# Storing the softmax statistics of a cross-attention kernel by quarters of the queries

## The chip, the cores and the metric

The kernel runs on one core of a Trainium2 chip. The metric is the device time of one execution in microseconds, as a median over runs. Its five engines are named as in the profile: PE (TensorE matmuls; PEld is its weight loading), DVE (VectorE), ACT (ScalarE), POOL (GpSimd) and SP (SyncE, which here only issues DMAs).

## What is computed

Two decoder layers on `x` of shape (2, 512, 1024), with a context of shape (2, 1024, 1024), all in float32. The first layer adds a quantized matrix product of the normalized `x` with the context, and a linear layer with routed LoRA. The second adds a cross-attention with 32 query heads over 8 key/value heads of width 128, and a linear layer with a top-1 LoRA. The change lies in the cross-attention of the second layer:

```python
q = (query @ wq).reshape(bs, sq, N_Q_HEADS, D_K).transpose((0, 2, 1, 3))
...
raw = jnp.einsum('bhqd,bhkd->bhqk', q, k) / scale
masked = raw + mask[:bs, None, curr_seq_pos:curr_seq_pos + sq, :sk]
attn = jax.nn.softmax(masked, axis=-1)
out = jnp.einsum('bhqk,bhkd->bhqd', attn, v)
out = out.transpose((0, 2, 1, 3)).reshape(bs, sq, N_Q_HEADS * D_V)
return out @ wo
```

With 2 batches and 32 heads there are 64 heads to work through. One has 512 queries and 1024 keys.

## The kernel before

Scores are kept transposed: keys lie on the 128 partitions, queries along the free dimension. A head's scores are eight blocks of 128 keys by 512 queries, in two SBUF tiles `e[0]` and `e[1]` of [128, 4, 512] (blocks, queries). The softmax statistics of a query, its maximum and its sum of exponentials, therefore need a reduction over blocks and then over partitions.

`Head.scores` (L763 to L784) does the products with PE and adds the mask on DVE, out of a two-bank PSUM tile `wide` into `e` (L782). `Head.tree` (L786 to L797) takes the maximum over the eight blocks with four DVE instructions: L790 of two halves of `e[0]` into a tile `m` of [128, 2, 512], L792 and L794 of `m` with the halves of `e[1]`, and L796, which folds `m` to its first [128, 512]. `over_partitions` (L727) finishes the reduction: it turns the 512 columns onto partitions by four PE transposes (L732; the data are PE's weights, the identity is what streams), and one DVE reduction (L734) gives [128, 4] numbers. `to_row` writes these to DRAM so that one transfer can bring them back as a row for all partitions (`from_row`, L747). To have that write in order, query 4p + t has to be at partition p, column t; so `over_partitions` views its input as "p (q t) -> p t q", and transpose number t takes every fourth query. The 128 weight columns of a transpose lie four floats, 16 bytes, apart.

`Head.exponential` (L812) subtracts the maximum on DVE (L814, out of PSUM, where ACT has put it at L810), takes the exponential on ACT (L817), and sums on POOL: for the first half of the keys L820 (`e[0]`'s two halves into a tile `d` of [128, 2, 512]), for the second L823 and L824 (`d` with each half of `e[1]`) and L825, which folds `d` to [128, 512]. `turn_sum` then runs `over_partitions` and a reciprocal (L805); POOL multiplies the result into the head's output at L842 (`normalize`). `Head.attend` (L827) is the product with the values (L831).

The order of all engines in this stage is the order of the program; no scheduler moves anything there. `attention` (L856) is a pipeline over heads with three phases per iteration n. In the first, head n + 2 has its scores made. In the second, PE runs three or four steps of the output projection of the group of four heads that is finished (L355, whose results DVE adds with L322 and L328 and POOL adds with L310), and DVE runs the tree of head n + 2 between those additions. In the third, PE runs in this order: the transposes for head n's sum, half of head n's product with the values, the transposes for head n + 2's maximum, and the other half; DVE, ACT and POOL work through the exponentials of head n + 1. Where a group of four heads is finished, POOL also makes the operands of its projection (`left_sums`, L242, lines L245 to L253). PE waits in its queue wherever a wait comes up, with everything behind it.

The queues: SP issues the loads of q, keys, values, masks and weights, ACT issues the two transfers of `row` (L741, L747).

Of the kernel before, what the change touches and what calls it, by code (L numbers as in the profile page):

```python
# [15 lines left out]
ALU = mybir.AluOpType  # L16
AX = mybir.AxisListType

P = 128
B, S, D = 2, 512, 1024  # L20
# [11 lines left out]
NT = S // P  # L32
# [7 lines left out]
def decoder_kernel(  # L40
# [25 lines left out]
    nc = tc.nc  # L66
# [8 lines left out]
    def new(shape, tag, bufs, dtype=F32):  # L75
        n_tiles[0] += 1
        return sb.tile(list(shape), dtype, tag=tag, name=f"{tag}_{n_tiles[0]}", bufs=bufs)
# [4 lines left out]
    def u4(shape, dtype=F32):  # L82
        return new(shape, "u4", 17, dtype)
# [4 lines left out]
    def small(shape):  # L88
        return new(shape, "small", 16)

    def ps_wide():
        n_tiles[0] += 1
        return ps.tile([P, D], F32, tag="wide", name=f"wide_{n_tiles[0]}", bufs=2)
# [23 lines left out]
    for name, ap in qparams.items():  # L117
        t = const.tile([P, 1], F32, name=f"qp_{name}")
        nc.gpsimd.dma_start(t, ap.partition_broadcast(P))
        qp[name] = t  # L120
    for side in ("x1", "x2"):
        t = const.tile([P, 1], F32, name=f"qp_inv_{side}")
# [603 lines left out]

    def over_partitions(src, op, negate=False):  # L727

        src = src.rearrange("p (q t) -> p t q", t=NT)
        tr = ps_wide()[:, 0:HALF].rearrange("p (t q) -> p t q", t=NT)  # L730
        for t in range(NT):
            nc.tensor.transpose(tr[:, t, :], src[:, t, :], ident)  # L732
        r = small([P, NT])
        nc.vector.tensor_reduce(r, tr, AX.X, op, negate=negate)  # L734
        return r

    def to_row(col):

        n_tiles[0] += 1
        row = dr.tile([S], F32, tag="row", name=f"row_{n_tiles[0]}", bufs=8)  # L740
        nc.scalar.dma_start(row.rearrange("(p t) -> p t", t=NT), col)  # L741
        return row
# [9 lines left out]
    class Head:  # L752
# [32 lines left out]

        def tree(self):  # L786

            e = self.e
            m = self.m = u4([P, 2, S])
            nc.vector.tensor_tensor(m, e[0][:, 0:2, :], e[0][:, 2:4, :], ALU.max)  # L790
            yield
            nc.vector.tensor_tensor(m, m, e[1][:, 0:2, :], ALU.max)  # L792
            yield
            nc.vector.tensor_tensor(m, m, e[1][:, 2:4, :], ALU.max)  # L794
            yield
            nc.vector.tensor_tensor(m[:, 0, :], m[:, 0, :], m[:, 1, :], ALU.max)  # L796
            yield  # L797

        def turn_maximum(self):
            self.nmx = over_partitions(self.m[:, 0, :], ALU.max, True)  # L800
            self.nmx = to_row(self.nmx)

        def turn_sum(self):
            den = over_partitions(self.d[:, 0, :], ALU.add)
            nc.vector.reciprocal(den, den)  # L805
            self.den = to_row(den)

# [4 lines left out]
        def exponential(self, j):  # L812
            e = self.e[j]
            nc.vector.tensor_tensor(  # L814
                e, e, self.nmf.unsqueeze(1).to_broadcast([P, 4, S]), ALU.add
            )
            nc.scalar.activation(e, e, AF.Exp)  # L817
            if j == 0:
                d = self.d = u4([P, 2, S])
                nc.gpsimd.tensor_tensor(d, e[:, 0:2, :], e[:, 2:4, :], ALU.add)  # L820
            else:
                d = self.d
                nc.gpsimd.tensor_tensor(d, d, e[:, 0:2, :], ALU.add)  # L823
                nc.gpsimd.tensor_tensor(d, d, e[:, 2:4, :], ALU.add)  # L824
                nc.gpsimd.tensor_tensor(d[:, 0, :], d[:, 0, :], d[:, 1, :], ALU.add)  # L825

        def attend(self, j):  # L827
            if j == 0:
# [27 lines left out]
    def attention(extra):  # L856
# [28 lines left out]
        for n in range(-2, total + GRP + 1):  # L885
# [30 lines left out]
            for _ in range(3 + k % 2 if n > GRP else 0):  # L916
                next(stretches, None)
                next(tree, None)
# [3 lines left out]
            for _ in range(extra.pop(n, 0)):  # L922
                for _ in range(2):
                    next(tree, None)
                next(extra["products"])
# [469 lines left out]
```

## Time and profile before

| | |
|---|---|
| median of 3 runs | 2449.82 us (2448.38 to 2452.53) |
| profiled execution, its own time | 2450.07 us |
| its span, first to last instruction | 2448.3 us |
| granted TensorE clock | 0.999 |
| PE busy | 2412.5 us (99%) |
| DVE busy | 1841.1 us (75%) |
| POOL busy | 1031.3 us (42%) |
| ACT busy | 530.8 us (22%) |
| L732, the transposes in `over_partitions` | 512, from 948.5 to 2302.7 us |
| L790, first instruction of the tree | 64, median 1.888 us |
| L820, L823, L824, sums of exponentials | 64 each, mean 2.367, 2.354, 2.356 us |

Busy shares are means over the whole span. Here they mix a first part of some 930 us, in which POOL has little to do, with the attention stage, from about 930 to 2310 us, in which POOL is busy 59 us of 83. A PE matmul's recorded duration contains a latency that overlaps with the next matmul, so PE's pace is read from the distance of two starts, or from the chain of waits, and not from the mean duration.

### The profile page before, as it was taken

Reading aid. Unit: us, or ns where it says so; the run is one execution under the profiler, and the core shown is the slowest. Engines: PE = TensorE matmul, PEld = TensorE weight load, DVE = VectorE, ACT = ScalarE, POOL = GpSimd, SP = SyncE. Lnnn points to the kernel's source line nnn. Section 1 sums busy time; section 2 is a strip of 40 time slices with the busy share of each in tenths; the row PEclk is TensorE's granted clock in tenths of the full one; section 3 lists DMA queues with packets and bytes.
Section 4 is the critical chain, followed back from the end, with each engine's and each line's share of the span. In section 5 each row is a group of like instructions: output and inputs, shape, how many; then the busy total and the mean of one; then the engine's idle time right before and its main releaser. Section 6 shows DMA issues by size and latency. Waiting matters only on the chain.

```text
span 2448.3 us, 19583 instructions
## 1 busy us (share of the span) xinstructions
PE 2412.5 (99%) x6792; PEld 1195.8 (49%) x6800; DVE 1841.1 (75%) x1994; ACT 530.8 (22%) x623; POOL 1031.3 (42%) x550
## 2 busy tenths in 40 slices
PE   8999999999999999999999999999999999999999
PEld 3477458654444443444444444444444444444444
DVE  4949774345876556898888888888898998888653
ACT  1210221011222222322222222222222222222210
POOL 0000010210000001677676767667776767677621
PEclk9999999999999999999999999999999999999999
DMA  5537133013796221244323323442433343233501
GB/s 182 181 105 273 69 134 108 26 60 116 274 330 216 78 91 56 77 156 111 81 83 107 114 65 90 142 145 79 125 116 79 94 125 112 66 90 108 172 9 60
DMA packets 149010, 288.01 MB, mean 118 GB/s; under 512 B 29424, under 2 KB 47360, under 8 KB 146608
## 3 DMA queue, kind: packets, MB, share of 16 engines
q1 hardware_dynamic: 108080, 244.35, 29.9%
q10 hardware_dynamic: 40400, 41.70, 6.9%
q8 instruction: 54, 0.88, 0.2%
q0 software_dynamic: 432, 0.71, 0.1%
q14 instruction: 44, 0.36, 0.1%
HBM read 223.54 MB, written 63.18 MB: 117 GB/s over the span
## 4 chain that ended last, share of the span: by engine, by line
PE 60%; DVE 6%; POOL 2%; issue 1%; DMA 1%; ACT 1%; ACTq 0%; SPq 0%; DVEq 0%; POOLq 0%
PE b L355 26%; PE wide L768 16%; PE b L831 15%; PE wide L732 2%; DVE u L814 2%; DMA u<-in_wo_dram 1%; DVE u L782 1%; POOL u L823 0%; POOL u L824 0%; DVE small L734 0%; DVE u L792 0%; DVE u L794 0%; ACT u L817 0%; POOL u L825 0%; DVE u L328 0%
## 5 line engine op out<-in xcount | busy, mean ns | idle before, releaser
L355 PE MATMUL b<-u,u 128*128 128x512 f32 (+1 forms) x3616 | 1394.2, 542 | 21.3 <-DMA u<-in_ctxT_in_dram 7.6
L355 PEld LDWEIGHTS b<-u,u 128*128 128x128 f32 x3616 | 684.6, 191 | 695.9 <-issue 612.8
L768 PE MATMUL wide<-u,u 128*128 128x512 f32 x1024 | 454.8, 595 | 7.3 <-DVE u L782 6.4
L831 PE MATMUL b<-u,u 128*128 128x512 f32 x1024 | 460.3, 592 | 0.0
L782 DVE TENSOR_TENSOR u<-wide,u 128x1024 f32<-128x1024 f32 x256 | 312.8, 1224 | 130.3 <-PE wide L768 129.9
L817 ACT ACTIVATE u<-u 128x2048 f32<-128x2048 f32 x128 | 244.7, 1912 | 655.8 <-DVE u L814 593.9
L768 PEld LDWEIGHTS wide<-u,u 128*128 128x128 f32 x1024 | 193.4, 190 | 257.3 <-issue 177.9
L814 DVE TENSOR_TENSOR u<-u,b 128x2048 f32<-128x2048 f32 x128 | 290.2, 2268 | 0.0
L820 POOL TENSOR_TENSOR u<-u 128x1024 f32<-128x1024 f32 x64 | 151.5, 2367 | 317.5 <-ACT u L817 310.1
L831 PEld LDWEIGHTS b<-u,u 128*128 128x128 f32 x1024 | 186.2, 192 | 184.6 <-issue 184.6
L310 POOL TENSOR_TENSOR u<-u,u 128x512 f32<-128x512 f32 x120 | 188.5, 1597 | 175.4 <-DVE u L322 153.2
L328 DVE TENSOR_TENSOR u<-u,b 128x512 f32<-128x512 f32 x200 | 135.8, 680 | 126.0 <-PE b L355 125.9
L222 POOL TENSOR_TENSOR u<-u,sin_t 128x512 f32<-128x512 f32 x8 | 11.6, 1456 | 402.7 <-ACT u L217 402.7
L823 POOL TENSOR_TENSOR u<-u,u 128x1024 f32<-128x1024 f32 x64 | 150.7, 2354 | 36.4 <-ACT u L817 36.0
L824 POOL TENSOR_TENSOR u<-u,u 128x1024 f32<-128x1024 f32 x64 | 150.8, 2356 | 5.0
L842 POOL TENSOR_TENSOR u<-u,u 128x512 f32<-128x512 f32 x64 | 119.9, 1873 | 10.0 <-DMA u<-row 10.0
L216 ACT ACTIVATE u<-u 64x512 f32<-64x512 f32 x72 | 45.2, 628 | 356.3 <-DVE u L293 177.6
L790 DVE TENSOR_TENSOR u<-u 128x1024 f32<-128x1024 f32 x64 | 115.8, 1810 | 0.0
L732 PEld LDWEIGHTS wide<-ident,u 128*128 128x128 f32 x512 | 79.6, 203 | 63.9 <-issue 55.0
L612 POOL TENSOR_TENSOR u<-u,u 128x1024 f32<-128x1024 f32 x8 | 20.2, 2529 | 214.9 <-DVE u L168 111.6
L792 DVE TENSOR_TENSOR u<-u,u 128x1024 f32<-128x1024 f32 x64 | 105.4, 1646 | 0.2
L825 POOL TENSOR_TENSOR u<-u 128x512 f32<-128x512 f32 x64 | 101.0, 1578 | 5.0
(135 smaller groups left out, 1614.3 us busy)
## 6 DMA issues: line engine op xcount, KB each, us to landing
u<-row ACTq DMA_DIRECT2D x128, 256.0 KB, 3.7
u<-wo SPq DMA_DIRECT2D x64, 512.0 KB, 4.0
u<-in_wo_dram SPq DMA_DIRECT2D x48, 512.0 KB, 4.5
u<-in_wq_dram SPq DMA_DIRECT2D x32, 512.0 KB, 4.2
q<-u SPq DMA_DIRECT2D x64, 256.0 KB, 2.4
u<-in_wo_dram SPq DMA_DIRECT2D x16, 1024.0 KB, 8.2
wo<-u SPq DMA_DIRECT2D x32, 512.0 KB, 4.2
u<-q SPq DMA_DIRECT2D x64, 256.0 KB, 4.2
```

What stands on the lines that cost most here:

```text
L310: nc.gpsimd.tensor_tensor(c, c, what, ALU.add)
L328: nc.vector.tensor_tensor(c, c, acc, ALU.add)
L355: nc.tensor.matmul(acc, lhsT, rhs, start=start and k == 0, stop=k == len(pairs) - 1, skip_group_check=True,)
L732: nc.tensor.transpose(tr[:, t, :], src[:, t, :], ident)
L768: nc.tensor.matmul(sc[:, ts(n, HALF)], self.kT[:, ts(2 * j + n, P)], self.qT, start=True, stop=True,)
L782: nc.vector.tensor_tensor(self.e[j // 2][:, js, :], sc.rearrange("p (k q) -> p k q", k=2), mask[j], ALU.add)
L814: nc.vector.tensor_tensor(e, e, self.nmf.unsqueeze(1).to_broadcast([P, 4, S]), ALU.add)
L817: nc.scalar.activation(e, e, AF.Exp)
L820: nc.gpsimd.tensor_tensor(d, e[:, 0:2, :], e[:, 2:4, :], ALU.add)
L823: nc.gpsimd.tensor_tensor(d, d, e[:, 0:2, :], ALU.add)
L824: nc.gpsimd.tensor_tensor(d, d, e[:, 2:4, :], ALU.add)
L831: nc.tensor.matmul(self.acc, self.v[:, k, :], self.e[j][:, k % 4, :], start=(k == 0), stop=(k == NKT - 1),)
```

## The change

`m` and `d`, the tiles that hold the tree's results and the sums, get the shape [128, 2, 4, 128]: the queries stand in them by quarters, t outermost. A new helper `by_quarter` views `e` in that order, "p k (q t) -> p k t q", and the instructions that read `e` (in the tree the first three, in the sums the first three) now read it with a step of four floats, and write or update `m` and `d` with neighbouring columns. L796 and L825 work on `m` and `d` alone, without gaps. `over_partitions` drops its view and takes `src[:, t, :]` as it stands, so that the 128 weight columns of each transpose are neighbours. The tiles have the same bytes as before, and no instruction is added, dropped or moved.

```diff
     def over_partitions(src, op, negate=False):
-        src = src.rearrange("p (q t) -> p t q", t=NT)
         tr = ps_wide()[:, 0:HALF].rearrange("p (t q) -> p t q", t=NT)
         for t in range(NT):
             nc.tensor.transpose(tr[:, t, :], src[:, t, :], ident)
...
+    def by_quarter(src):
+        return src.rearrange("p k (q t) -> p k t q", t=NT)
...
         def tree(self):
-            e = self.e
-            m = self.m = u4([P, 2, S])
-            nc.vector.tensor_tensor(m, e[0][:, 0:2, :], e[0][:, 2:4, :], ALU.max)
+            e = [by_quarter(half) for half in self.e]
+            m = self.m = u4([P, 2, NT, P])
+            nc.vector.tensor_tensor(m, e[0][:, 0:2], e[0][:, 2:4], ALU.max)
             yield
-            nc.vector.tensor_tensor(m, m, e[1][:, 0:2, :], ALU.max)
+            nc.vector.tensor_tensor(m, m, e[1][:, 0:2], ALU.max)
             yield
-            nc.vector.tensor_tensor(m, m, e[1][:, 2:4, :], ALU.max)
+            nc.vector.tensor_tensor(m, m, e[1][:, 2:4], ALU.max)
             yield
-            nc.vector.tensor_tensor(m[:, 0, :], m[:, 0, :], m[:, 1, :], ALU.max)
+            nc.vector.tensor_tensor(m[:, 0], m[:, 0], m[:, 1], ALU.max)
             yield
...
             nc.scalar.activation(e, e, AF.Exp)
+            e = by_quarter(e)
             if j == 0:
-                d = self.d = u4([P, 2, S])
-                nc.gpsimd.tensor_tensor(d, e[:, 0:2, :], e[:, 2:4, :], ALU.add)
+                d = self.d = u4([P, 2, NT, P])
+                nc.gpsimd.tensor_tensor(d, e[:, 0:2], e[:, 2:4], ALU.add)
             else:
                 d = self.d
-                nc.gpsimd.tensor_tensor(d, d, e[:, 0:2, :], ALU.add)
-                nc.gpsimd.tensor_tensor(d, d, e[:, 2:4, :], ALU.add)
-                nc.gpsimd.tensor_tensor(d[:, 0, :], d[:, 0, :], d[:, 1, :], ALU.add)
+                nc.gpsimd.tensor_tensor(d, d, e[:, 0:2], ALU.add)
+                nc.gpsimd.tensor_tensor(d, d, e[:, 2:4], ALU.add)
+                nc.gpsimd.tensor_tensor(d[:, 0], d[:, 0], d[:, 1], ALU.add)
```

More of the change, by code (lines that the diff above doesn't have):

```diff
@@ L786, in tree @@
         def tree(self):
-            e = self.e
-            m = self.m = u4([P, 2, S])
-            nc.vector.tensor_tensor(m, e[0][:, 0:2, :], e[0][:, 2:4, :], ALU.max)
+            e = [by_quarter(half) for half in self.e]
+            m = self.m = u4([P, 2, NT, P])
+            nc.vector.tensor_tensor(m, e[0][:, 0:2], e[0][:, 2:4], ALU.max)
             yield
-            nc.vector.tensor_tensor(m, m, e[1][:, 0:2, :], ALU.max)
+            nc.vector.tensor_tensor(m, m, e[1][:, 0:2], ALU.max)
             yield
-            nc.vector.tensor_tensor(m, m, e[1][:, 2:4, :], ALU.max)
+            nc.vector.tensor_tensor(m, m, e[1][:, 2:4], ALU.max)
             yield
-            nc.vector.tensor_tensor(m[:, 0, :], m[:, 0, :], m[:, 1, :], ALU.max)
+            nc.vector.tensor_tensor(m[:, 0], m[:, 0], m[:, 1], ALU.max)
             yield
         def turn_maximum(self):
-            self.nmx = over_partitions(self.m[:, 0, :], ALU.max, True)
+            self.nmx = over_partitions(self.m[:, 0], ALU.max, True)
             self.nmx = to_row(self.nmx)
         def turn_sum(self):
-            den = over_partitions(self.d[:, 0, :], ALU.add)
+            den = over_partitions(self.d[:, 0], ALU.add)
             nc.vector.reciprocal(den, den)
```

## The prediction

> **What bounds the kernel now.** I read the page first: engine shares, then the chain of work that ended last.
>
> ```profile
> PE 2412.5 (99%) x6792; PEld 1195.8 (49%) x6800; DVE 1841.1 (75%) x1994; ACT 530.8 (22%) x623; POOL 1031.3 (42%) x550
> PE b L355 26%; PE wide L768 16%; PE b L831 15%; PE wide L732 2%; DVE u L814 2%; DMA u<-in_wo_dram 1%; DVE u L782 1%; POOL u L823 0%; POOL u L824 0%; DVE small L734 0%; DVE u L792 0%; DVE u L794 0%; ACT u L817 0%; POOL u L825 0%; DVE u L328
> ```
>
> PE is the bound; the transposes (L732) are 2% of the chain, and DVE and POOL lines of the softmax appear in it here and there, so they are near it. Next, the chain in order of time, for one head in the middle of attention (start, length, what):
>
> ```profile
> 1503.84 0.47 PE wide L732 x4
> 1504.31 3.44 PE b L831 x8
> 1507.75 0.47 PE wide L732 x4
> 1508.22 3.44 PE b L831 x8
> 1511.65 6.87 PE wide L768 x16
> 1518.52 6.87 PE b L355 x16
> ```
>
> No gap: PE goes from one matmul to the next, and a head lasts 21.54 us (19.83 where the projection has three steps). Whatever PE saves is saved, and whatever makes PE wait is lost in full. So I looked next at how late the two transposes' inputs are. On DVE the tree, then in PE's timeline the transposes of the maximum that wait for it:
>
> ```profile
> 1520.88 1.34 DVE L790 TENSOR_TENSOR u<-u 128x1024 f32<-128x1024 f32 x1
> 1522.74 1.69 DVE L792 TENSOR_TENSOR u<-u,u 128x1024 f32<-128x1024 f32 x1
> 1524.95 1.70 DVE L794 TENSOR_TENSOR u<-u,u 128x1024 f32<-128x1024 f32 x1
> 1527.17 1.16 DVE L796 TENSOR_TENSOR u<-u 128x512 f32<-128x512 f32 x1
> 1529.13 0.63 PE L732 MATMUL wide<-ident,u 128*128 128x128 f32 x4
> ```
>
> The tree ends at 1528.33, 0.80 us before PE takes it. In four heads in a row the same distance is 0.28, 0.47, 0.80 and 0.87 us; the shortest anywhere in the stage is about 0.15, which is the handover itself. That leaves 0.13, 0.32, 0.65 and 0.72 us to spare: DVE has almost none. POOL, before the transposes of the sum at 1503.68:
>
> ```profile
> 1488.58 3.74 POOL L310 TENSOR_TENSOR u<-u,u 128x512 f32<-128x512 f32 x3
> 1492.50 2.37 POOL L820 TENSOR_TENSOR u<-u 128x1024 f32<-128x1024 f32 x1 [0.17 <-ACT u L817]
> 1495.35 2.36 POOL L823 TENSOR_TENSOR u<-u,u 128x1024 f32<-128x1024 f32 x1 [0.48 <-ACT u L817]
> 1497.78 2.35 POOL L824 TENSOR_TENSOR u<-u,u 128x1024 f32<-128x1024 f32 x1
> 1500.21 2.13 POOL L825 TENSOR_TENSOR u<-u 128x512 f32<-128x512 f32 x1
> 1503.68 0.63 PE L732 MATMUL wide<-ident,u 128*128 128x128 f32 x4
> ```
>
> The sum is ready at 1502.34, 1.34 us early, 1.28 beyond a handover of 0.06. The next three heads have 4.09, 2.72 and 4.78. In this head POOL was without work for only 0.17 us before L820: from the previous head's L842 on it had made the projection's operands and three additions.
>
> **What the change takes from PE.** The loads of transposes with neighbouring columns can be seen in the same trace, at L204 (nanoseconds: least, median, most):
>
> ```profile
> L732 PEld LDWEIGHTS wide<-ident,u x512: 195/207/223, 948.5 to 2302.7; 128*128 128x128 f32 x171
> L204 PEld LDWEIGHTS wide<-ident,u x192: 139/141/143, 361.3 to 2382.7; 128*128 128x128 f32 x192
> 361.56 1.04 PE L204 MATMUL wide<-ident,u 128*128 128x128 f32 x8
> 362.43 7.07 PE L355 MATMUL b<-u,u 128*128 128x256 f32 x32
> ```
>
> A load shrinks by 66 ns, which over 512 would be 34 us, but loads overlap matmuls. What counts is pace: L204's eight start 0.87 us before the next matmul, 0.109 each; L732's four take 0.47 on the chain, 0.1175 each. Four save 0.47 - 4 x 0.109 = 0.035 us. There are 128 groups of four: 4.5 us, 0.18% of the span. I bound it at 0 and at 5.5 (a group at 0.427, the pace of 128 columns at a fourth of L831's 0.429 per matmul). Everything else is the price.
>
> **What it puts on DVE.** L790, L792 and L794 read `e` in steps of 16 bytes; L790 does so with both operands. The trace has no such DVE read. Below nothing is excluded: the elements are as many. The nearest row is PE's own: a load of 128 columns 16 bytes apart every 0.1175 us is 0.92 ns per column, while DVE needs 1.02 ns per element (L790's least 1.215 us for 1024, L796's least 0.691 for 512). By that row a stepped read keeps up and the tree costs nothing more. Against it stands the Trainium skill, "SBUF — State Buffer", section "Door 1: The DMA port swizzle": SBUF works in 16-byte lines, and each access that goes to a new line pays a penalty[...]. It gives no price; a doubled stream would be 1.05 us on each of three instructions, X = 3.1 us. PE would then wait X less the spare: 4 x 3.1 - 1.8 = 10.6 us in four heads, 169 us in 64. By the row 0, by the rule up to 169. I take the row, as it is this chip reading with this very step, and keep the other end for the range. The gain is eaten already at X = 0.36 us: (0.36 - 0.13) + (0.36 - 0.32) = 0.27 per four heads, which is what PE saves there (8 x 0.035).
>
> **What it puts on POOL.** L820, L823 and L824 read `e` in the same steps. Again no row shows it; below nothing is excluded in the same way. PE's row would let it pass: POOL takes 2.12 ns per element ((2.355 - 1.271 us) / 512), more than twice 0.92. The rule: the Trainium skill, "GPSIMD Engine Reference", section "7. Performance pitfalls for Q7 kernels": an SBUF read that steps by more than 8 bytes takes about 2.9 cycles per element in place of 1.9. Here I take the rule, since it was measured on this engine and PE's load tells of PE's port alone. One cycle at the page's 1.2 GHz is 0.83 ns: an estimate of 0.85 us for each of the three instructions, Y = 2.55 us per head. Ends: 0, and 7.1 (all three twice as long).
>
> Where this ends, by the four heads: POOL works through the fourth head's sums, then L842, the operands and three additions, and L820 of the next head follows with 0.17 us of slack. So that head gets the delay twice: 2 x 2.55 - 0.17 - 1.28 = 3.65 us of waiting PE. The other three have 4.03, 2.66 and 4.72 to spare and cover 2.55.
>
> There is a second path. DVE and POOL hold each other up when both read two operands from SBUF:
>
> ```profile
> L790 DVE TENSOR_TENSOR u<-u x64: 1215/1888/3348, 939.9 to 2256.3; 128x1024 f32<-128x1024 f32 x64
> ```
>
> The most, 3.35, is the least plus 2.13: it stood behind a POOL instruction. A later L824 now reaches into the tree. In the head shown L790 (1520.88) would wait for L824 to end at 1519.77 + 2.55 = 1522.3 and end near 1523.4 instead of 1522.22: 1.2 late, less 0.65 to spare, 0.5. The next head's L824 ends at 1540.99 + 2.55 = 1543.5, so L790 ends at 1544.6 instead of 1543.41: 1.2 less 0.72, again 0.5. In the fourth L824 ends at 1563.3, where L790 already waited to. Together 1.0. L328, L796 and the subtractions (L814) queue behind the tree on DVE, and ACT's exponentials behind L814, so a late tree delays the next sums too; that is the same wait once more and I don't add it.
>
> Sum: 3.65 + 1.0 = 4.65 us per four heads, times 15 (the first group has no operands to make) = 70; less 4.5: 65 us. Against the profiled execution's 2450.07 (span 2448.3 and 1.8 around it; 0.25 above the median) that is 2515 us.
>
> **No cost.** L796 and L825 stay contiguous and as long. SP's and ACT's transfers are the same: `row` gets the same bytes in the same order. All engines' instructions keep number and place, so no queue is passed and no buffer lives longer, except by the delays above.
>
> **The rivals.** *Nobody pays.* Stepped reads run at full pace on DVE and POOL. Then only the 4.5 us remain: 2445.5. For it: PE's 0.92 ns per column. Against: POOL's page. Chance 0.25. *DVE pays* (alone, or with POOL). 3.1 us more in the tree gives 169 - 4.5: 2615 us; it decides from X = 0.36 on, and in that case POOL's delay lies mostly beside it, since the wait for the sum gives the tree time. With half the price, X = 1.55, (1.42 + 1.23 + 0.90 + 0.83) x 16 = 70. For it: the line rule, and a tree with 0.13 us to spare. Against: PE's row. Chance 0.33. *The change doesn't do what it says*: columns become neighbours but the transposes keep their pace; L204 speaks against it, and it would only take the 4.5 us away.
>
> **How the numbers follow.** POOL alone pays: 0.42, 2515 us, with 2465 to 2600 for Y from 1.5 to 4.7. A measurement of this kernel tells about 0.2%, 5 us, from no change. Nobody pays: its 4.5 lie just within that; I give 0.09 to faster, 0.14 to same and 0.02 to slower. Of POOL's case 0.02 is same (a price under Y = 0.9 stays below PE's gain), 0.40 slower; DVE's 0.33 is slower. Together 0.09, 0.16 and 0.75. The range from 2444 to 2640 takes in the case of no price and DVE's doubled reads; outside lie about 0.04 below and 0.12 above (both engines paying double, each standing behind the other).
>
> **What would show it.** Right: L732's loads at 0.14 us and four transposes at 0.435 on the chain; L820 to L824 at 3.2 us or more; PE waiting for POOL's L825 ahead of the sum's transposes, in every fourth head first, up to 3.6 us; the tree's least times still 1.215. Wrong: L790's least well above 1.3 us (DVE pays, and PE waits for L796 in every head), or L820 still at 2.37 (then only PE's gain is left). It would be wrong in size if both engines are slow and stand behind each other more than I counted.

## The result and the profile after

The changed kernel takes 2707.7 us (median; 2706.2 to 2713.6) against 2449.1 us: a ratio of 1.105, 95% interval 1.104 to 1.107, 258 us slower. The prediction was slower at 2515 us, with a range up to 2640; the time lies outside it. In the changed kernel's lines the transposes are L731, the tree L793, L795, L797 and L799, the sums L824, L827, L828 and L829, POOL's multiplication L846, the product with the values L835, and DVE's subtraction and ACT's exponential L817 and L820.

The page of the changed kernel, span, busy times and the chain that ended last:

```profile
span 2706.9 us, 19591 instructions
PE 2474.1 (91%) x6800; PEld 1202.9 (44%) x6800; DVE 2102.6 (78%) x1994; ACT 530.2 (20%) x623; POOL 1397.2 (52%) x550
PE 31%; POOL 21%; DVE 15%; issue 4%; ACT 2%; DMA 1%; POOLq 0%; ACTq 0%; SPq 0%; DVEq 0%
```

And the chain's shares before:

```profile
PE 60%; DVE 6%; POOL 2%; issue 1%; DMA 1%; ACT 1%; ACTq 0%; SPq 0%; DVEq 0%; POOLq 0%
```

The span grew by 258.6 us. PE is busy 61.6 us longer and idle 197.0 us longer. PE was 60% of the chain before; now POOL and DVE together hold more of it than PE does. The single instructions, from the views of their lines (nanoseconds: least, median, most):

```profile
L731 PEld LDWEIGHTS wide<-ident,u x512: 137/141/231, 946.7 to 2561.3; 128*128 128x128 f32 x171
L793 DVE TENSOR_TENSOR u<-u x64: 1990/3028/4732, 938.2 to 2509.0; 128x1024 f32<-128x1024 f32 x64
L795 DVE TENSOR_TENSOR u<-u,u x64: 2002/2524/4541, 940.2 to 2511.9; 128x1024 f32<-128x1024 f32 x64
L797 DVE TENSOR_TENSOR u<-u,u x64: 2020/2486/2983, 942.3 to 2516.1; 128x1024 f32<-128x1024 f32 x64
L824 POOL TENSOR_TENSOR u<-u x64: 4051/4169/4255, 971.0 to 2547.9; 128x1024 f32<-128x1024 f32 x64
L827 POOL TENSOR_TENSOR u<-u,u x64: 2857/2878/2933, 975.2 to 2552.0; 128x1024 f32<-128x1024 f32 x64
```

The loads shrank as expected, to L204's 141 ns. All three tree instructions need 2.0 us at least where 1.215 did before, whether one operand is stepped or both. POOL needs 1.80 us more where both are (2.367 before) and 0.52 more where one is (2.354). Two rows of the page show what else grew, POOL instructions that the change doesn't touch (busy, mean ns, then idle before):

```profile
L846 POOL TENSOR_TENSOR u<-u,u 128x512 f32<-128x512 f32 x64 | 187.7, 2934 | 11.2 <-DMA u<-row 11.2
L829 POOL TENSOR_TENSOR u<-u 128x512 f32<-128x512 f32 x64 | 160.8, 2513 | 5.0
```

Before, these were 1.873 us (L842) and 1.578 us (L825). They stand behind DVE's longer reads, as the run with the tree alone will show. And PE's transposes, with its idle time ahead of them and who ended it, after and before:

```profile
L731 PE MATMUL wide<-ident,u 128*128 128x128 f32 x512 | 88.2, 299 | 176.4 <-POOL u L829 128.5 <-DVE u L799 44.4 <-DVE u L206 2.0
L732 PE MATMUL wide<-ident,u 128*128 128x128 f32 x512 | 81.8, 282 | 2.7 <-POOL u L825 1.6 <-DVE u L796 0.9
```

The chain in order of time, through one head and into the next (start, length, what):

```profile
1659.86 2.40 DVE u L797
...
1663.71 2.27 DVE u L817
...
1666.00 1.92 ACT u L820
...
1667.99 4.20 POOL u L824
...
1678.17 2.93 POOL u L829
...
1694.99 4.17 POOL u L824
...
1706.81 2.90 POOL u L829
...
1709.75 1.12 PE wide L731 x4
1710.87 5.13 PE b L835 x8
1716.00 0.44 PE wide L731 x4
1716.43 3.44 PE b L835 x8
```

It runs from the tree through the exponential into POOL, through two heads' sums there, and only then to PE. The last four lines show the gain, four transposes in 0.44 us in place of 0.47, and something new: after its wait PE takes 1.12 and 5.13 us for what otherwise takes 0.44 and 3.44. The stretches around that wait have the reason (the columns are busy times, then the granted clock):

```profile
core 0: us, PE busy (x) PEld busy (x) DVE busy (x) ACT busy (x) POOL busy (x), PEclk, DMA share, GB/s
1704.00:1709.70 5.70, 0.00 (x0) 0.00 (x0) 5.70 (x5) 0.00 (x0) 5.62 (x3) 0.79 0.04 14
1709.70:1713.20 3.50, 3.45 (x7) 1.92 (x8) 3.46 (x3) 0.00 (x0) 2.98 (x1) 0.50 0.00 0
1713.20:1716.00 2.80, 2.80 (x8) 1.26 (x7) 2.77 (x4) 0.00 (x0) 0.00 (x0) 0.83 0.03 1
1716.00:1720.00 4.00, 4.00 (x13) 1.99 (x12) 3.11 (x3) 2.52 (x2) 1.76 (x1) 1.00 0.59 123
```

PE's clock falls to half in the wait and stays there for some microseconds of work. That is where most of the 61.6 us of longer busy time are: the products with the values, which follow these waits, alone are busy 44.8 us longer (after, then before):

```profile
L835 PE MATMUL b<-u,u 128*128 128x512 f32 x1024 | 505.1, 640 | 0.0
L831 PE MATMUL b<-u,u 128*128 128x512 f32 x1024 | 460.3, 592 | 0.0
```

### The profile page after: what moved, and what is told of

It is laid out like the page before. It is cut to its first block, busy times and chain, and to the rows that moved or that the text cites. A ratio compares the mean times of both kernels' runs of the same rounds, so it can differ in the third digit from the quotient of the medians.

```text
span 2706.9 us, 19591 instructions
## 1 busy us (share of the span) xinstructions
PE 2474.1 (91%) x6800; PEld 1202.9 (44%) x6800; DVE 2102.6 (78%) x1994; ACT 530.2 (20%) x623; POOL 1397.2 (52%) x550
## 4 chain that ended last, share of the span: by engine, by line
PE 31%; POOL 21%; DVE 15%; issue 4%; ACT 2%; DMA 1%; POOLq 0%; ACTq 0%; SPq 0%; DVEq 0%
PE b L355 14%; PE wide L771 7%; PE b L835 7%; POOL u L824 5%; POOL u L828 4%; POOL u L827 4%; DVE u L795 3%; DVE u L797 3%; POOL u L829 3%; DVE u L817 2%; POOL u L310 2%; ACT u L820 1%; DVE u L328 1%; POOL u L846 1%; PE wide L731 1%
## 5 line engine op out<-in xcount | busy, mean ns | idle before, releaser
L355 PEld LDWEIGHTS b<-u,u 128*128 128x128 f32 x3616 | 683.1, 191 | 719.1 <-issue 605.1
L835 PE MATMUL b<-u,u 128*128 128x512 f32 x1024 | 505.1, 640 | 0.0
L820 ACT ACTIVATE u<-u 128x2048 f32<-128x2048 f32 x128 | 244.6, 1911 | 902.7 <-DVE u L817 865.5
L824 POOL TENSOR_TENSOR u<-u 128x1024 f32<-128x1024 f32 x64 | 266.8, 4169 | 253.5 <-ACT u L820 253.5
L835 PEld LDWEIGHTS b<-u,u 128*128 128x128 f32 x1024 | 203.0, 209 | 213.0 <-issue 213.0
L817 DVE TENSOR_TENSOR u<-u,b 128x2048 f32<-128x2048 f32 x128 | 290.1, 2268 | 0.0
L310 POOL TENSOR_TENSOR u<-u,u 128x512 f32<-128x512 f32 x120 | 200.2, 1694 | 174.0 <-DVE u L322 152.9
L731 PE MATMUL wide<-ident,u 128*128 128x128 f32 x512 | 88.2, 299 | 176.4 <-POOL u L829 128.5
L328 DVE TENSOR_TENSOR u<-u,b 128x512 f32<-128x512 f32 x200 | 136.1, 681 | 125.4 <-PE b L355 120.1
L828 POOL TENSOR_TENSOR u<-u,u 128x1024 f32<-128x1024 f32 x64 | 225.9, 3530 | 5.0
L793 DVE TENSOR_TENSOR u<-u 128x1024 f32<-128x1024 f32 x64 | 199.6, 3119 | 0.0
L795 DVE TENSOR_TENSOR u<-u,u 128x1024 f32<-128x1024 f32 x64 | 195.8, 3059 | 0.2
L846 POOL TENSOR_TENSOR u<-u,u 128x512 f32<-128x512 f32 x64 | 187.7, 2934 | 11.2 <-DMA u<-row 11.2
L827 POOL TENSOR_TENSOR u<-u,u 128x1024 f32<-128x1024 f32 x64 | 184.3, 2879 | 5.3 <-ACT u L820 0.4
L731 PEld LDWEIGHTS wide<-ident,u 128*128 128x128 f32 x512 | 63.4, 151 | 261.2 <-POOL u L829 155.8
L829 POOL TENSOR_TENSOR u<-u 128x512 f32<-128x512 f32 x64 | 160.8, 2513 | 5.0
L797 DVE TENSOR_TENSOR u<-u,u 128x1024 f32<-128x1024 f32 x64 | 158.8, 2481 | 0.1
```

Source lines behind the costliest of these rows:

```text
L310: nc.gpsimd.tensor_tensor(c, c, what, ALU.add)
L355: nc.tensor.matmul(acc, lhsT, rhs, start=start and k == 0, stop=k == len(pairs) - 1, skip_group_check=True,)
L795: nc.vector.tensor_tensor(m, m, e[1][:, 0:2], ALU.max)
L817: nc.vector.tensor_tensor(e, e, self.nmf.unsqueeze(1).to_broadcast([P, 4, S]), ALU.add)
L824: nc.gpsimd.tensor_tensor(d, e[:, 0:2], e[:, 2:4], ALU.add)
L827: nc.gpsimd.tensor_tensor(d, d, e[:, 0:2], ALU.add)
```

## The experiments

The theory after the result: DVE and POOL both pay for reads in steps of 16 bytes, the two prices add, and PE's half clock adds to them. The rival: POOL alone pays, as predicted, and DVE's longer times are waiting behind POOL.

**The tree alone.** Only DVE reads by quarters.

```diff
-            e = by_quarter(e)
...
-                d = self.d = u4([P, 2, NT, P])
+                d = self.d = u4([P, 2, S])
...
-            den = over_partitions(self.d[:, 0], ALU.add)
+            den = over_partitions(self.d[:, 0, :], ALU.add, turned=False)   # views it "p (q t) -> p t q"
```

> Only the tree's three instructions on DVE read by quarters; the sums on POOL and their transposes are as before. Theory (DVE and POOL both pay for reads in steps of 16 bytes, 0.79 us more for each DVE instruction of 1024 elements): the tree takes 2.4 us more, of which about 0.45 was to spare, so PE waits near 1.9 us per head, about 120 us in 64 heads, and POOL's instructions that stand behind a DVE read get longer: 2550 to 2600 us. Rival 'POOL alone' (DVE's longer times in the changed kernel are only waiting behind POOL): DVE's least times stay 1.215 us and the time is 2447 to 2455 us.

Measured: 2577.0 us, ratio 1.052 (1.050 to 1.053), 127 us more. The tree's first instruction, and POOL's multiplication (L842 before, least 1.258, median 2.248 us):

```profile
L795 DVE TENSOR_TENSOR u<-u x64: 1996/2541/4079, 940.1 to 2381.4; 128x1024 f32<-128x1024 f32 x64
L847 POOL TENSOR_TENSOR u<-u,u x64: 1267/3072/3131, 1008.1 to 2440.0; 128x512 f32<-128x512 f32 x64
```

DVE needs 2.0 us with POOL reading as before: the price is DVE's own, 0.78 us per instruction, and the rival falls. By the prediction's own account, X = 2.37 (0.775 + 0.784 + 0.81) less the spare, 4 x 2.37 - 1.82 = 7.66 us per four heads, gives 123 us in 64, or 121 after PE's gain of 2.2 in its 64 shorter groups. The total fits better than its parts: in the trace PE waits 80.6 us for the tree itself,

```profile
PE wide L733 <- DVE u L801: 80.6, 55, 4.2
```

(us in all, times, longest), and 13.1 us more for DVE's additions (L328), which stand in DVE's queue among the tree's instructions. POOL's multiplication is 1.8 us over its least where it stands behind a DVE read; before it was 1.0. With its own instructions unchanged, POOL is busy 1177.1 us here for 1031.3.

**The sums alone.** Only POOL reads by quarters.

```diff
-            e = [by_quarter(half) for half in self.e]
-            m = self.m = u4([P, 2, NT, P])
+            e = self.e
+            m = self.m = u4([P, 2, S])
...
-            self.nmx = over_partitions(self.m[:, 0], ALU.max, True)
+            self.nmx = over_partitions(self.m[:, 0, :], ALU.max, True, turned=False)
```

> Only the sums on POOL read by quarters; the tree and the maximum's transposes are as before. Theory: POOL takes 1.80 + 0.52 + 0.53 = 2.85 us more per head; by the prediction's own account 2 x 2.85 - 1.45 = 4.25 us of waiting in every fourth head and about 1.2 through the tree, 15 groups, 80 us, and some more if PE's clock falls after the waits: 2525 to 2560 us. Rival 'POOL alone': nearly all of the 258 us is here, 2690 us or more. If the two effects only lay beside each other, this would be near the changed kernel less a few us.

Measured: 2573.3 us, ratio 1.050 (1.049 to 1.052), 123 us more. So each price is there alone, and they add to 127 + 123 = 250 of 258; the rival, which has nearly all of it here, falls again. PE's wait in every fourth head, in its timeline:

```profile
1461.71 1.12 PE L733 MATMUL wide<-ident,u 128*128 128x128 f32 x4 [4.13 <-POOL u L831]
1462.62 4.61 PE L837 MATMUL b<-u,u 128*128 128x512 f32 x8
```

With Y = 2.85 the prediction's 2Y - 1.45 is 4.25 us; it is 4.13, in just this head of four. But the sum was above the 2525 to 2560 expected; the slow transposes (1.12) and products behind the wait suggest why.

**Is PE's half clock on the path?** First in the changed kernel:

```diff
+        wide = ps_wide()
+        for _ in range(fill):      # 2 to 6 in 33 heads, ahead of the sum's transposes
+            nc.tensor.matmul(wide[:, HALF:D], ident, mask[0][:, 0, :], start=True, stop=True)
```

> The changed kernel with idle matmuls (identity by a block of the mask, 0.86 us each, into the unused half of the transposes' PSUM tile; their result is used nowhere) put ahead of the sum's transposes, two to six of them in the 33 heads in which PE waited 1.9 to 5.9 us there; none fills more than its wait. Theory (PE's clock is granted at half after such a wait, and the 4 transposes and first matmuls behind it run slow on the path that sets the end): no slow stretch is left, about 2.2 us less in each of the some 22 heads with long waits, 2645 to 2665 us, and PE's granted clock back at 0.99 or more. Rival (DVE and POOL set the pace all the same, so a slow PE is hidden behind them): 2700 to 2715 us.

Measured: 2697.1 us, ratio 1.101 (1.100 to 1.103). The granted clock came back, 0.994 for 0.972, but only 10 us with it. My theory fell here: behind the wait for the sum PE, faster now, comes to its next wait that much earlier. Without the idle matmuls' own 118.7 us it is busy 48.3 us less (2425.8 for 2474.1), but it stands still 36.1 us longer, the filling counted (268.9 for 232.8): for DVE's additions L328 37.3 us where it was 20.0, for the sum, with the filling, 149.5 where it was 128.5, while the waits for the tree stay (43.5, 44.4). DVE and POOL set the pace from one head to the next. Then in the kernel with only the sums by quarters, where PE waits for the tree only once:

```diff
+    FILL = {3: 4, 5: 2, 9: 4, 13: 4, 17: 4, 21: 4, 25: 4, 29: 4, 33: 4, 37: 4, 39: 2, 41: 3, 45: 4, 49: 4, 53: 4, 57: 4, 61: 4}
...
-            den = over_partitions(self.d[:, 0], ALU.add)
+            den = over_partitions(self.d[:, 0], ALU.add, fill=FILL.get(NH * self.b + self.hd, 0))
```

> The kernel with only the sums by quarters, with idle matmuls (2 to 4, result used nowhere) in the 17 heads in which PE waited 2.4 to 4.2 us for the sum. In the changed kernel such matmuls brought only 10 us of 258, since the tree made the next wait anyway. Theory (here the tree is as fast as before, so behind the wait PE sets the pace again, and half clock costs its own time): about 2 us less in 15 heads, 2540 to 2550 us against 2573. Rival (POOL sets the pace in these heads from one to the next, and PE's loss is hidden here too): 2565 us or more.

Measured: 2546.5 us, ratio 1.039 (1.037 to 1.040), 27 us less than without the idle matmuls. The timeline around the fill (L735 is the fill):

```profile
1448.82 3.60 PE L735 MATMUL wide<-u,ident 128*128 128x512 f32 x8
1453.13 0.66 PE L738 MATMUL wide<-ident,u 128*128 128x128 f32 x4 [0.71 <-POOL u L836]
1453.62 3.60 PE L842 MATMUL b<-u,u 128*128 128x512 f32 x8
```

So half clock costs its own time where PE sets the pace after the wait, and little where it doesn't. POOL's price without it is 96 us. The prediction's terms with Y = 2.85 come near that: L824 ends 2.85 us later, so L790 ends 1.5, 1.5 and 0.3 us later in the three heads, 1.8 beyond their spare; the head with 2.66 to spare lacks 0.19; and 15 x (4.25 + 1.8 + 0.19) = 94, or 91 after PE's gain of 2.2. But that is partly luck, as PE's waits with only the sums by quarters show:

```profile
PE wide L733 <- POOL u L831: 76.8, 32, 4.2
PE wide L733 <- DVE u L801: 2.4, 1, 2.4
```

PE waits for the tree once, where the sum has 1.8 us in each of 15 groups. Instead it waits for POOL's sum a second time in each group, two heads after the long wait and mostly for 0.4 to 1.5 us. POOL does hold the tree up (L790's median is 2.66 us there for 1.89). In the chain of the run with idle matmuls the tree stands ahead of the exponential and the next two heads' sums, and only these reach PE, so the delay seems to go that way; no run takes it apart further.

**Is it the step, or the line?** Halves in place of quarters: steps of 8 bytes (`m` and `d` are then [128, 2, 2, 256]).

```diff
     def by_quarter(src):
-        return src.rearrange("p k (q t) -> p k t q", t=NT)
+        return src.rearrange("p k (q u) -> p k u q", u=2)
...
+        src = src.rearrange("p u (q v) -> p v u q", v=2)
-            nc.tensor.transpose(tr[:, t, :], src[:, t, :], ident)
+            nc.tensor.transpose(tr[:, t, :], src[:, t // 2, t % 2, :], ident)
```

> Tree and sums keep their results by halves of the queries (even, odd) in place of quarters: DVE and POOL read in steps of 8 bytes, two elements to a 16-byte line, and the transposes' weight columns lie 8 bytes apart. Theory (what costs is an access that takes only one element from a 16-byte line): the tree's least times are 1.215 us and POOL's 2.37 again, and the time is 2445 us if PE's loads at 8 bytes keep the pace of neighbouring columns, 2449 if they don't. Rival (any step costs, since a read no longer takes neighbours): the tree's least near 2.0 us, POOL's sums up, 2600 to 2710 us.

Measured: 2450.1 us, ratio 1.000 (0.999 to 1.001). From its lines:

```profile
L794 DVE TENSOR_TENSOR u<-u x64: 1214/1638/3206, 941.0 to 2261.1; 128x1024 f32<-128x1024 f32 x64
L825 POOL TENSOR_TENSOR u<-u x64: 2810/2840/2852, 973.9 to 2295.8; 128x1024 f32<-128x1024 f32 x64
L828 POOL TENSOR_TENSOR u<-u,u x64: 2377/2392/2402, 976.8 to 2298.7; 128x1024 f32<-128x1024 f32 x64
L732 PEld LDWEIGHTS wide<-ident,u x512: 194/204/219, 949.5 to 2310.0; 128*128 128x128 f32 x171
```

DVE reads two elements of each 16-byte line and pays nothing. POOL pays 0.47 us with two stepped operands, where I expected nothing, and 0.04 with one, which its slack takes. The Trainium skill, "GPSIMD Engine Reference", section "7. Performance pitfalls for Q7 kernels", has a price only for steps above 8 bytes; with two stepped operands this run has one at 8. PE's load is as slow at 8 bytes as at 16 (204 ns, 207), so there is nothing to gain this way. On DVE the result fits the theory of lines. The Trainium skill, "SBUF — State Buffer", section "Door 1: The DMA port swizzle", asks for at least two accesses to each 16-byte line for full bandwidth: with two elements to a line the read was free, with one it cost 0.78 us. The same passage gives 4 fp32 as how far one can stride for free; read as a step of four elements, that is not what DVE did. A step of 12 bytes was not tried, so whether the line or the length of the step decides, and where the price begins, is open.

**Getting the gain without stepped reads of `e`.** Four tries. In the first, transposes take the columns as they stand, and ACT and POOL undo the row's other order where they read it.

```diff
-        src = src.rearrange("p (q t) -> p t q", t=NT)
+        src = src.rearrange("p (t q) -> p t q", t=NT)
...
-            nc.scalar.copy(self.nmf, self.nmx)
+            nc.scalar.copy(self.nmf.rearrange("p (t q) -> p t q", t=NT), self.nmx.rearrange("p (q t) -> p t q", t=NT))
...
-            nc.gpsimd.tensor_tensor(self.oT, self.oT, self.den, ALU.mult)
+            nc.gpsimd.tensor_tensor(o, o, den, ALU.mult)    # o "p (t q) -> p t q", den "p (q t) -> p t q"
```

> Tree and sums stay in the queries' order and the transposes take neighbouring columns as they stand, so the row in DRAM is in another order; this is undone where the row is used, by a stepped read on ACT (the copy of the maximum into PSUM) and on POOL (the multiplication by the reciprocal of the sum). DVE reads nothing in steps. Theory: PE saves its 0.035 us in 128 groups, 4.5 us; POOL's multiplication costs about 0.26 us more (half of 0.52 for half the elements) and ACT's copy under 0.5, both with room: 2444 to 2446 us. Rival: the 0.26 us delay the operands of the projection and the next sums in every fourth head, where POOL has 0.17 us idle and 1.28 to spare, and the stepped read on ACT holds up L814's input: 2449 us or more.

Measured: 2453.6 us, ratio 1.0015 (1.0008 to 1.0021), the rival's case. PE's busy time fell by 5.1 us, to 2407.4, and its waits ahead of the transposes rose from 2.7 to 11.3: POOL's multiplication takes 0.26 us more at least (1.514), and ACT's copy 1.11 us for 0.59. The second leaves POOL alone:

```diff
+            den = u2([P, S])
+            nc.scalar.copy(den.rearrange("p (t q) -> p t q", t=NT), self.den.rearrange("p (q t) -> p t q", t=NT))
+            nc.gpsimd.tensor_tensor(self.oT, self.oT, den, ALU.mult)
```

> As the run with the row turned back by ACT and POOL, but ACT turns back both rows (one more ACT copy of 512 elements per head, about 1.1 us, into a tile of its own), and POOL's multiplication reads neighbours as before the change. Theory (the 4.5 us were lost again to POOL's 0.25 us per head, which is passed on to the sum's transposes): PE's waits for POOL ahead of the sum's transposes fall back to 2 or 3 us in all and the time is 2444 to 2447 us. Rival (ACT's longer copies delay the copies of PSUM banks, L320, which PE and DVE wait for): 2450 us or more, with DVE's L322 waiting for ACT.

Measured: 2453.6 us, ratio 1.0008 (0.9999 to 1.0016). PE's waits ahead of the transposes fell to 5.9 us, but DVE's addition L322 stood 21.9 us behind ACT's copy of the maximum (L810; 10.9 before), and PE 7.4 us behind ACT's copy L320 (2.5 before). Both theory and rival were seen; the gain is eaten, and which of these waits took how much of it was not separated.

The third lets the transfer put the row in order.

```diff
-        nc.scalar.dma_start(row.rearrange("(p t) -> p t", t=NT), col)
+        nc.scalar.dma_start(row.rearrange("(t p) -> p t", t=NT), col)
```

> As in the run with the row turned back by ACT and POOL, the tree and the sums stay in the queries' order and the transposes take neighbouring columns; here the transfer that writes the row puts it in order, 512 pieces of 4 bytes in place of 128 of 16. No engine reads or writes in steps. Theory: the row has time (its maximum is written some 8 us before its return is used, the sum's more), so PE keeps all of the 4.5 us: 2445 us. Rival: the small pieces make the write last so long, or ACT's queue take so long to issue it, that L810 and L814 or the POOL multiplication come late: 2452 us or more.

Measured: 2888.3 us, ratio 1.179 (1.177 to 1.181), a clear miss. The row's write, from the view of its line, and that of before from the list of transfers (KB, median us to landing):

```profile
DMA to landing us min/median/max: 7.8/10.1/15.6
```

```profile
row<-small ACTq DMA_DIRECT2D x128, 2.0 KB, 3.0
```

The write takes 10.1 us in place of 3.0, and ACT, which issues the read-back in its own queue, stands still behind it: its copy of the product (L839) waits 521.2 us in all for it (20.8 before), and PE waits 205.1 us for ACT's copy L320 (2.5 before). I had counted only the row's own slack, not what stands behind the waiting ACT.

The fourth writes by quarters in the last instruction, and reads neighbours everywhere.

```diff
-            nc.vector.tensor_tensor(m[:, 0, :], m[:, 0, :], m[:, 1, :], ALU.max)
+            f = self.f = u2([P, NT, P])
+            nc.vector.tensor_tensor(f.rearrange("p t q -> p q t"), m0, m1, ALU.max)   # m0, m1: m's halves, "p (q t) -> p q t"
...
-                nc.gpsimd.tensor_tensor(d[:, 0, :], d[:, 0, :], d[:, 1, :], ALU.add)
+                g = self.g = u2([P, NT, P])
+                nc.gpsimd.tensor_tensor(g.rearrange("p t q -> p q t"), d0, d1, ALU.add)    # d0, d1: d's halves, likewise
```

> Tree and sums stay in the queries' order up to their last instruction; these two (512 elements, DVE's maximum and POOL's sum) read neighbours and write by quarters into a tile of their own, in steps of 512 bytes from element to element, and the transposes take neighbouring columns. Theory (a line costs where only one element of it is used, reads and writes alike): DVE's fold takes 0.4 us more, from 0.69 to 1.08 at least, against 0.13 us to spare, so PE waits about 0.5 us in four heads, less the 0.28 saved: 2450 to 2460 us. Rival (writes in steps are free): 0.69 stays, 2445 us.

Measured: 2453.3 us, ratio 1.0014 (1.0007 to 1.0021). The folds (before: 0.691 and 1.264 us at least):

```profile
L796 DVE TENSOR_TENSOR u<-u x64: 1039/1064/1997, 943.7 to 2265.2; 128x512 f32<-128x512 f32 x64
L829 POOL TENSOR_TENSOR u<-u x64: 1275/1286/2150, 980.1 to 2300.0; 128x512 f32<-128x512 f32 x64
```

DVE pays for stepped writes about as for reads, 0.35 us for 512 elements (half of the read's 0.78 is 0.39). POOL doesn't. That suggests the version that does only POOL's half:

```diff
-            den = over_partitions(self.d[:, 0, :], ALU.add)
+            den = over_partitions(self.g, ALU.add, turned=True)    # the maximum's columns still "p (q t) -> p t q"
```

> Only POOL's last addition writes the sum by quarters into a tile of its own, which the run with both folds showed to cost it nothing (least 1.275 us for 1.264); the tree and the maximum's transposes are as before. Theory: 64 of the 128 groups of transposes save 0.035 us, 2.2 us in all, 2447 to 2448 us, about 0.1%, at the edge of what five rounds can tell. Rival (the tile added to a pool of ten makes other buffers wait, as the 22 us that DVE's L322 waited for ACT in the last run show that small delays are passed on): 2450 us or more.

Measured: 2446.7 us, ratio 0.9985 (0.9979 to 0.9992). This is 0.15% below the kernel before, some 3.5 us (2.0 to 5.1 by the interval) where 2.2 were expected. Its chain has one short group of transposes per head, the sum's, and one as before:

```profile
1521.39 0.44 PE wide L733 x4
1521.83 3.44 PE b L836 x8
1525.26 0.47 PE wide L733 x4
```

## Why the prediction was wrong, step by step

*What bounds the kernel, and the spare.* Right, in the total. Four heads' spare of 0.13, 0.32, 0.65 and 0.72 us, put against the tree's measured 2.37 us, gives 121 us after PE's gain, and the tree alone cost 127; 80.6 of these were seen as waiting for the tree.

*What PE gains.* Right: 0.44 us per group for 0.435.

*What DVE pays.* This is the step that failed: "I take the row, as it is this chip reading with this very step". PE's load told nothing of DVE. The value taken as 0 was 2.37 us: 0.78, 0.78 and 0.81 on three instructions. The rule of the 16-byte lines, which I set aside, gave the right answer for DVE at this step; that a line needs two accesses, so that a step of 8 bytes is free, I had left out. The price was three quarters of the doubled stream that I had put at the far end (3.1). DVE's case had a chance of 0.33 and 2615 us.

*What POOL pays.* It pays, as the rule said. The total came near by luck: 2.85 us for 2.55, but made of 1.80, 0.52 and 0.53 in place of 0.85 three times. The long wait came in the head that was named, at 4.13 us for 3.65.

*The two together.* Also wrong: "POOL's delay lies mostly beside it". The chain shows them in series: tree, exponential, sums, the next transposes. Tree and sums alone cost 127 and 123, both 258. That this adds up so well is partly chance: 27 of the 123 are PE's half clock, which costs only 10 when both are there. With the clock filled up the sums cost 96 and both together 247, 24 more than 127 + 96, which comes only when both engines are slow. Had the smaller lain beside the larger, the time would have been near 2577 us, inside the range.

*Waiting for each other.* The mechanism was right, its place was not, and one direction of it was left out. I counted POOL's longer reads in front of the tree, 1.0 us of PE's waiting in four heads, and did not add the delay of the next sums. With only the sums by quarters it was the other way round: PE waited for the tree once, and for a second sum in each group. DVE's longer reads in front of POOL weigh as much as POOL's own: POOL is busy 82.0 us in four heads (of 100.1) where it was 59.1 (of 83.0), 22.9 more. Its own reads make 4 x 2.85 = 11.4 of that; the other 11.5 are time in which its instructions stand behind DVE.

*PE's clock.* Not in the prediction. It costs 27 us in the kernel with only the sums by quarters, and about 10 in the changed kernel.

*The chances.* The direction was right: 0.75 for slower. The upper bound left out both engines paying and holding each other up, which was given about 0.12.

## What to carry to other kernels

A layout change moves its stepped access to another engine, so price it on that engine: here PE paid 8.7 ns per 128 columns, (0.47 - 0.435) / 4, and DVE 780 ns per 1024 elements for the same step. Where no row of that engine exists, don't take the other engine's row as its price; keep the dearer end in the sum until the trace says otherwise. When two engines in one pipeline both get slower, look along the chain whether they stand in series before letting one cover the other, and look for a place where a step is free, as POOL's write was here.

## What the hardware showed that was not expected

- DVE at fp32: 1.215 us for 1024 elements in steps of 4 or 8 bytes, 1.97 to 2.02 in steps of 16, the same for one stepped operand and two. A write in steps of 512 bytes cost about as much per element, 0.35 us for 512.
- POOL: 1.80 us more for 1024 elements with both operands in steps of 16 bytes, 0.52 with one (0.47 and 0.04 in steps of 8); a write of 512 elements in steps of 512 bytes cost 0.01.
- ACT: a copy of 512 elements that reads SBUF in steps of 16 bytes and writes PSUM takes 1.11 us for 0.59.
- PE's granted clock: in the wait shown, PE stood still from 1703.9 to 1709.75 us. The clock was 1.00 until 1707.0, 0.82 in the half microsecond after that and 0.50 from 1707.5 on, so it fell some 3.4 us into the wait; it was back at 1.00 at 1714.2, some 4.4 us after work had begun again. The Trainium skill, "TensorE: Matmul & The Clock Gate", section "Part 1: The HAM clock gate", has half clock after an idle window of about 3.4 us, which this agrees with. With only the tree by quarters, where most waits are of 1.3 to 1.6 us, the mean clock stayed at 0.995. Whether half clock costs time depended on who set the pace after the wait.
- A row of 512 numbers written to DRAM in 4-byte pieces took 10.1 us for 3.0 in 16-byte pieces.
